# Four graph layers on one core: layer 3's q and k as seven block products, its attention one chunk further behind

## The chip, the core and the metric

The kernel runs on one core of a Trainium2 chip. The metric is the device time of one launch in microseconds, the median of several runs. In the profile the engines are PE (TensorE, matrix products; PEld is its loading of weights), DVE (VectorE), ACT (ScalarE), POOL (GpSimd) and SP (SyncE, which in this kernel only issues transfers). SBUF is the memory on the chip that all engines read and write, PSUM the eight banks into which TensorE writes its products, and DRAM the memory outside.

## What is computed

`x` is 128 batches x 64 tokens x 256 features, all float32. Four layers follow one another; each takes `h = max(layernorm(x), 0)` and adds its result to `x`. Layer 0 is a graph convolution with batch normalisation, layer 1 two graph convolutions and four small LSTMs. The change touches only layers 2 and 3:

```python
# layer 2: one head, causal, over the 64 tokens of a batch
q, k, v = split(h @ Wqkv)
scores = einsum('btd,bsd->bts', q, k) / sqrt(256) + adj_mask        # -1e30 above the diagonal
y = einsum('bts,bsd->btd', softmax(scores), v)
x = x + y @ Wo

# layer 3: four heads of 64, masked by the graph
q, k, v = (h @ W), cut into 3 parts and 4 heads
scores = einsum('bhid,bhjd->bhij', q, k) / sqrt(64) + mask          # mask: -inf where adj is 0
x = x + einsum('bhij,bhjd->bhid', softmax(scores), v)
```

## The kernel before

The 8192 tokens are 16 chunks of 512 (8 batches). Layers 0 and 1 end at 1545.8 us of the profiled execution; the rest is layers 2 and 3, chunk by chunk. They are made of small steps, Python functions in a table `steps`, each of which takes a chunk's number. The order of the work is written out by hand in strings: `FIRST` for chunks 0 to 2, `ROUND` for each of the chunks 3 to 12, `NORM` for 13 and 14, `LAST` for 15. `exp3-2` in a round for chunk c is the step exp3 of chunk c-2, `q2+0` the step q2 of chunk c. `run` (L1436) calls the steps in that order, and the schedule is manual: every engine, SP too, executes its instructions in the order of the string. An engine whose next instruction has to wait holds up all that stands behind it on that engine, while the others go on. Each kind of tile has a fixed number of buffers in a pool (two in pool `l2` where nothing else is said), and a step that takes the next buffer waits until the one before last has been read. All matrix products and transposes of layers 2 and 3 take their bank of PSUM from one ring of eight (`bank`), in the order of the calls.

Layer 2 of a chunk. Its two weights are folded ahead of time: `wqk_sb` is Wq times Wk transposed, so there is no k, and `wvo_sb` is Wv times Wo. The steps, with the engine and the name of their lines in the profile:

- load2: four transfers fetch the activations in channel layout (features on the partitions, tokens along).
- q2: four matmuls of 512 columns into two banks (L1108); ACT copies the first half of q to SBUF, DVE the second (copyq2).
- v2a, v2b: four matmuls of 256 columns each (L1101), an ACT copy each.
- score2: 16 small matmuls (L1191, tile 128x64); DVE scales, adds the mask, and takes the row maximum; POOL subtracts it (`shifted`, L1113). exp2 on ACT; divide2: sums, reciprocal and product on DVE.
- turn2: two transposes on TensorE (L1135) and an ACT copy. out2: 32 small matmuls (L1222, tile 64x32), and DVE adds the result to the residual `xs[c]`.
- keep: `put` sends `xs[c]` to DRAM; back reads it into another token order (four transfers), as layer 3's output will need it.

Layer 3 of a chunk:

- norm3: layer norm's statistics on DVE, then 1/sqrt on POOL. apply3: normalise and max on ACT. square3: DVE re-orders 32x32 squares, and a `put` and, in load3, four reads from DRAM complete the transposition into channel layout. chan3 does the same with eight TensorE transposes and two copies; it is used for chunks 0, 1 and 15, where no time lies between apply and use.
- q30, k30, q31, k31 (`qk3`, L1250): halves of q and k, two matmuls of 512 columns each into a bank of their own; ACT copies three of them to SBUF, DVE the fourth.
- v3a, v3b as in layer 2. score3: 32 matmuls of 64x64 into two banks (L1275); DVE masks them (L1281) and takes the maximum, POOL subtracts.
- exp3 on ACT, sum3 and divide3 on DVE, turn3: eight transposes and two ACT copies; out3: 32 matmuls of 64x64 into two banks (L1322). store: DVE adds the residual, and a transfer writes the chunk's result.

In `LAST` the last chunk's softmax and products go in two halves (names ending in a and b). A round of before is:

```python
ROUND = """exp3-2 q2+0 copyq2+0 sum3-2 load3-1 load2+1 v2a+0 divide3-2 score2+0 exp2+0 v2b+0 divide2+0
           turn3-2 q30-1 turn2+0 out3-2 out2+0 keep+0 norm3+0 k30-1 store-2 q31-1 back+0 apply3+0
           k31-1 v3a-1 square3+0 score3-1 v3b-1"""
```

so layer 3's projections and scores run one chunk behind layer 2, and its softmax and output two chunks behind. `NORM` is the same for chunks 13 and 14, whose followers come to layer 2 by norm2, apply2 and chan2 (on DVE, POOL, ACT and TensorE) in place of load2. `differences` (L671) belongs to the LSTMs: there a 2x2 block product is made of seven block matmuls, and POOL or DVE makes four differences of the operand's blocks for it. `put` (L231) uses a ring of four DRAM buffers for all of these trips.

## Time and profile before

| | us |
|---|---|
| median of 3 runs (lowest, highest) | 1932.98 (1932.7, 1933.74) |
| the profiled execution, whole | 1931.83 |
| its span, first to last instruction | 1929.9 |
| layers 0 and 1 | 0 to 1545.8 |
| layers 2 and 3 | 1545.8 to 1929.9, 384.1 |
| a steady round of them | 23.23 |
| LAST | 1879.92 to 1929.9, 49.98 |

How to read the lines that follow. The page's first part gives each engine's busy time, its share of the span and its number of instructions. `PEclk` shows the clock that TensorE was granted in 40 slices of the span, in tenths (9 is full or nearly so). A line of windows gives, for one stretch, its length, the busy time of each engine with the number of instructions, the granted clock, the share of the DMA engines' time and their GB/s. A line of the timeline gives the start, the duration, the engine, the line of the code, the operation with its tiles and shape, and the number of records taken together. Durations of neighbouring groups overlap a little, since matmuls are pipelined, so what a group costs is the step from its start to the next start.

### The profile page before, as it was taken

How to read it: one execution, taken by the hardware profiler on the slowest of the kernel's cores; microseconds unless marked ns; L12 is line 12 of the kernel's file. 1: busy time of each engine (PE TensorE's matmuls, PEld its weight loads, DVE VectorE, ACT ScalarE, POOL GpSimd, SP SyncE). 2: the span in 40 equal slices, each digit the busy share in tenths (PEclk: the TensorE clock that was granted, in tenths of full speed). 3: DMA queues.
4: the chain of work that ended last, by engine and by line, in shares of the span. 5: the costliest groups of instructions: out<-in, count | busy, mean ns of one | idle time of the engine just before them, and what ended most of it. 6: DMA issues, size and time to landing. Idle time of an engine off the chain costs nothing.

```text
span 1929.9 us, 37881 instructions
## 1 busy us (share of the span) xinstructions
PE 1911.8 (99%) x14827; PEld 1434.3 (74%) x14827; DVE 1140.6 (59%) x2985; ACT 950.3 (49%) x2120; POOL 371.8 (19%) x553
## 2 busy tenths in 40 slices
PE   9999999999999999999999999999999999999998
PEld 5444465897897898799689789878979966666666
DVE  6544354546557656655755755665555566666675
ACT  5654434445456455455545545545555544334443
POOL 3205210221211221121121121112112111111121
PEclk9999999999999999999999999999999999999999
DMA  4216712225424522531632452353134154444432
GB/s 137 63 35 223 282 44 68 81 83 170 148 83 157 182 84 70 188 106 70 213 115 83 165 174 83 132 178 112 58 131 147 51 153 122 136 138 136 143 114 81
DMA packets 109058, 238.23 MB, mean 123 GB/s; under 512 B 11216, under 2 KB 73168, under 8 KB 108880
## 3 DMA queue, kind: packets, MB, share of 16 engines
q1 hardware_dynamic: 108128, 234.47, 36.7%
q8 instruction: 117, 1.92, 0.4%
q0 software_dynamic: 320, 1.05, 0.2%
q14 instruction: 61, 0.50, 0.1%
q10 hardware_dynamic: 432, 0.30, 0.1%
HBM read 168.93 MB, written 66.85 MB: 122 GB/s over the span
## 4 chain that ended last, share of the span: by engine, by line
PE 96%; DVE 2%; ACT 1%; issue 0%; POOL 0%; DVEq 0%; POOLq 0%; ACTq 0%
PE x L829 22%; PE g L793 17%; PE z L829 11%; PE z L347 6%; PE v L1101 6%; PE y L829 6%; PE z L364 6%; PE p_q L1108 5%; PE p_k L1108 3%; PE u L574 3%; PE v L560 3%; PE agg_a L201 1%; PE agg_c L201 1%; PE s L1275 1%; PE o L1322 1%; PE tr L1135 1%
## 5 line engine op out<-in xcount | busy, mean ns | idle before, releaser
L838 DVE TENSOR_TENSOR gates<-gates,x 128x128 f32<-128x128 f32 (+2 forms) x384 | 119.6, 323 | 337.1 <-PE x L829 330.1
L829 PE MATMUL x<-xd,wset 128*128 128x128 f32 (+2 forms) x1280 | 285.2, 311 | 0.4 <-DVE gates L838 0.2
L829 PE MATMUL x<-hd,wset 128*128 128x128 f32 (+2 forms) x1152 | 246.8, 303 | 0.0
L829 PEld LDWEIGHTS x<-xd,wset 128*128 128x128 f32 x1280 | 202.1, 190 | 17.8 <-DVE gates L838 4.1
L721 ACT ACTIVATE gates<-gates,bias 128x256 f32<-128x256 f32 (+4 forms) x384 | 170.5, 491 | 67.1 <-DVE gates L838 64.2
L887 POOL TENSOR_TENSOR gates<-gates 128x512 f32<-128x512 f32 (+2 forms) x48 | 75.0, 1562 | 647.9 <-ACT gates L721 647.9
L829 PEld LDWEIGHTS x<-hd,wset 128*128 128x128 f32 x1152 | 185.1, 191 | 5.0
L772 ACT ACTIVATE gates<-g,bias 128x512 f32<-128x512 f32 (+2 forms) x240 | 138.1, 610 | 97.9 <-PE g L793 94.6
L793 PE MATMUL g<-hT,wset 128*128 128x256 f32 (+2 forms) x744 | 184.4, 405 | 1.1 <-DVE hT L732 1.1
L793 PEld LDWEIGHTS g<-hT,wset 128*128 128x128 f32 x744 | 140.5, 190 | 44.1 <-issue 8.8
L793 PE MATMUL g<-hT,wih 128*128 128x512 f32 x384 | 166.4, 592 | 0.0
L835 ACT COPY gates<-y 128x128 f32<-128x128 f32 (+2 forms) x192 | 54.2, 294 | 205.1 <-PE y L829 204.7
L829 PE MATMUL z<-hs,wset 128*128 128x128 f32 (+2 forms) x768 | 154.1, 303 | 0.0
L793 PEld LDWEIGHTS g<-hT,wih 128*128 128x128 f32 x384 | 72.3, 190 | 87.7 <-issue 83.2
L829 PEld LDWEIGHTS z<-hs,wset 128*128 128x128 f32 x768 | 119.8, 191 | 3.3
L347 PE MATMUL z<-agg,w_sb 128*128 128x512 f32 x256 | 114.1, 598 | 0.1
L364 PE MATMUL z<-h,w_sb 128*128 128x512 f32 x256 | 110.2, 592 | 0.0
L778 DVE TENSOR_TENSOR cell<-gates 128x512 f32<-128x512 f32 (+2 forms) x80 | 50.5, 648 | 101.0 <-ACT gates L772 100.9
L838 DVE TENSOR_TENSOR gates<-gates,z 128x128 f32<-128x128 f32 (+2 forms) x384 | 104.9, 317 | 0.1
L835 ACT COPY gates<-x 128x128 f32<-128x128 f32 (+2 forms) x192 | 56.6, 296 | 93.7 <-PE x L829 93.0
L721 ACT ACTIVATE gates<-x,bias 128x128 f32<-128x128 f32 (+2 forms) x192 | 74.8, 390 | 50.9 <-PE x L829 48.0
L829 PE MATMUL z<-hT,wset 128*128 128x128 f32 (+1 forms) x512 | 96.9, 301 | 0.0
(211 smaller groups left out, 3544.9 us busy)
## 6 DMA issues: line engine op xcount, KB each, us to landing
wset<-wfar SPq DMA_DIRECT2D x96, 960.0 KB, 6.4
hT<-far_h SPq DMA_DIRECT2D x116, 128.0 KB, 2.9
far_h<-hm SPq DMA_DIRECT2D x16, 512.0 KB, 3.4
far_n<-xs SPq DMA_DIRECT2D x16, 512.0 KB, 6.3
xs<-far_n SPq DMA_DIRECT2D x64, 128.0 KB, 3.6
far_x<-xs SPq DMA_DIRECT2D x16, 512.0 KB, 2.6
x<-far_x SPq DMA_DIRECT2D x64, 128.0 KB, 3.4
xt<-in_x_dram SPq DMA_DIRECT2D x15, 512.0 KB, 4.0
```

The source lines that it names most:

```text
L347: nc.tensor.matmul(ps, w1_sb[:, k, m * P : (m + 1) * P], agg[:, k, :], start=(k == 0), stop=(k == KD - 1))
L364: nc.tensor.matmul(banks[c, m], w2_sb[:, k, m * P : (m + 1) * P], h1[c][:, k, :], start=(k == 0), stop=(k == KH - 1))
L560: nc.tensor.matmul(banks[m], wg0_sb[:, k, m * P : (m + 1) * P], agg[:, k, :], start=(k == 0), stop=(k == KD - 1))
L721: nc.scalar.activation(gate(q, c, part), src, AF.Tanh if q == 2 else AF.Sigmoid, bias=bs[:, q * KD + c : q * KD + c + 1])
L772: nc.scalar.activation(columns_of(gate(q, c)), natural(banks[q, c][:, :n].rearrange("p (w b) -> p w b", b=nb)), AF.Tanh if q == 2 else AF. ...
L793: nc.tensor.matmul(banks[q, c][:, :n].rearrange("p (w b) -> p w b", b=nb)[:, w, :], block(q, c, k), hv[:, k, w.start * p : (w.stop - 1) * ...
L829: nc.tensor.matmul(folded(self.psum(kind)), wsets[p, self.q][:, BLOCKS[kind][i], :], (ox[self.s] if part == "x" else oh)[kind], start=firs ...
L835: nc.scalar.copy(gate(self.q, kind // 5, halves[kind // 5]), self.psum(kind))
L838: nc.vector.tensor_add(gate(self.q, *dst), gate(self.q, *a), self.psum(kind))
L887: nc.gpsimd.tensor_mul(gates[:, 0, :, :n], gates[:, 0, :, :n], gates[:, 2, :, :n])
L1101: nc.tensor.matmul(ps[:, i, :], hT[:, k, j, :], w[:, k, first : first + D], start=(k == 0), stop=(k == KD - 1))
L1108: nc.tensor.matmul(ps.rearrange("p (a n) -> p a n", n=P), w[:, k, m * P : (m + 1) * P], hT[:, k], start=(k == 0), stop=(k == KD - 1))
```

## The change

Three things change together.

1. Layer 3 runs one chunk further behind. In the round for chunk c, its softmax and output are those of chunk c-3, its q, k and v those of chunk c-2, and its scores those of c-2 at the round's end. The strings are re-written for that: FIRST ends earlier, `LAST` no longer contains layer 2 of chunk 15, and the steps stand in another order. In a round, layer 3's output products (out3) now stand directly ahead of its scores; norm3 is cut in two (norm3a, norm3b) with the statistics of two of the four tiles in each; back reads the chunk put two rounds before. chan3 remains for chunk 0 alone; chunks 1 and 15 go through DRAM (square3, load3) like the others. `put` has twelve DRAM buffers where it had four. The pool of layer 1's right side is closed after FIRST, and a pool `l3` with two buffers takes its place for layer 3's new tiles, its v among them.

2. q and k of chunks 1 to 14 are made by seven block products. The operand is cut into 2x2 blocks: two halves of the features by two halves of the tokens. POOL forms four differences of activation blocks per chunk (`sums_h`), and once four combinations of weight blocks (`ring_places`, after FIRST). Each product is two matmuls of 256 columns (one for q, one for k) that share an accumulating bank: products 1, 6, 7 and 4 go into a bank X one after the other, 5 and 3 into Y, 2 into Z. ACT copies X or Y to its place in `qk` after products 1, 5, 6 and 4, and DVE adds Z, Y and X to what stands there (c11, c12, qc). The order of the steps is

       qa   product 2 -> Z, product 1 -> X, ACT: copy X
       q5   product 5 -> Y, ACT: copy Y                       (after layer 2's transposes, turn2)
       c11  DVE: add Z
       qb   product 6 -> X, ACT: copy X, product 3 -> Y
       qc   product 7 -> X, DVE: add X
       c12  DVE: add Y
       qd   product 4 -> X, ACT: copy X

   Chunks 0 and 15 keep q30, k30, q31 and k31.

3. `LAST` holds what is left: attention of chunk 13, projections, scores and attention of chunks 14 and 15.

The diff, without unchanged context:

```diff
-    def put(mid, name, tag="far", bufs=4):
+    def put(mid, name, tag="far", bufs=12):
...
         for k in range(2):
             steps["qk"[k] + f"3{m}"] = lambda c, m=m, k=k: qk3(c, m, k)
+    l3 = []
+    def ring_places():
+        pool = l3[0]
+        l3.append(pool.tile([P, 2, 4, P], F32, tag="ws", name="ws3", bufs=1))
+        a = w3_sb[:, :, : 2 * D].rearrange("p k (i m f) -> p k m i f", i=2, m=KD)
+        d = l3[1].rearrange("p i s f -> p s i f")
+        for dst, x, y, op in ((0, a[:, 0, 1], a[:, 1, 1], OP.add), (1, d[:, 0], a[:, 0, 0], OP.subtract),
+                              (2, a[:, 0, 0], a[:, 0, 1], OP.subtract),
+                              (3, a[:, 1, 0], d[:, 1], OP.subtract)):
+            nc.gpsimd.tensor_tensor(d[:, dst], x, y, op)
+    @step
+    def sums_h(c):
+        hT = st[c, "hT3"]
+        t = l3[0].tile([P, 4, CH // 2], F32, tag="td", name=f"td_{c}", bufs=1)
+        t = [t[:, i, :].rearrange("p (a n) -> p a n", n=P) for i in range(4)]
+        b = {(k, j): hT[:, k, 2 * j : 2 * j + 2, :] for k in range(KD) for j in range(2)}
+        for f in differences(nc.gpsimd, t, b[0, 0], b[0, 1], b[1, 0], b[1, 1]):
+            f()
+        st[c, "o7"] = {1: b[0, 0], 2: b[1, 0], 3: b[1, 1], 4: t[3], 5: t[0], 6: t[1], 7: t[2]}
+    def seven(c, kind, tag):
+        first = (c, tag) not in st
+        if first:
+            st[c, tag] = bank(f"{tag}7_{c}")
+        for i in range(2):
+            m, k = {1: (0, 0), 2: (0, 1), 4: (1, 1)}.get(kind, (0, 0))
+            w = (w3_sb[:, k, i * D + m * P : i * D + (m + 1) * P] if kind in (1, 2, 4) else
+                 l3[1][:, i, {5: 0, 6: 1, 7: 2, 3: 3}[kind], :])
+            nc.tensor.matmul(
+                st[c, tag][:, i * CH // 2 : (i + 1) * CH // 2].rearrange("p (a n) -> p a n", n=P), w,
+                st[c, "o7"][kind], start=first and not i, stop=True, skip_group_check=True)
+    def part7(c, m, j):
+        return st[c, "qk"][:, :, m, j * CH // 2 : (j + 1) * CH // 2]
+    def bank7(c, tag):
+        return st[c, tag].rearrange("p (i n) -> p i n", i=2)
+    @step
+    def qa(c):
+        st[c, "qk"] = l3[0].tile([P, 2, KD, CH], F32, tag="qk", name=f"qk_{c}", bufs=1)
+        seven(c, 2, "Z")
+        seven(c, 1, "X")
+        nc.scalar.copy(part7(c, 0, 0), bank7(c, "X"))
+    @step
+    def q5(c):
+        seven(c, 5, "Y")
+        nc.scalar.copy(part7(c, 1, 1), bank7(c, "Y"))
+    @step
+    def c11(c):
+        nc.vector.tensor_add(part7(c, 0, 0), part7(c, 0, 0), bank7(c, "Z"))
+    @step
+    def qb(c):
+        seven(c, 6, "X")
+        nc.scalar.copy(part7(c, 0, 1), bank7(c, "X"))
+        seven(c, 3, "Y")
+    @step
+    def c12(c):
+        nc.vector.tensor_add(part7(c, 0, 1), part7(c, 0, 1), bank7(c, "Y"))
+    @step
+    def qc(c):
+        seven(c, 7, "X")
+        nc.vector.tensor_add(part7(c, 1, 1), part7(c, 1, 1), bank7(c, "X"))
+    @step
+    def qd(c):
+        seven(c, 4, "X")
+        nc.scalar.copy(part7(c, 1, 0), bank7(c, "X"))
+        st[c, "q3"], st[c, "k3"] = st[c, "qk"][:, 0], st[c, "qk"][:, 1]
+    @step
+    def norm3a(c):
+        t = [small.tile([P, NJ, i], F32, tag=f"ln_{i}_4", name=f"st{i}_n3_{c}") for i in (6, 2)]
+        st[c, "stats"] = t
+        stats_of(c, range(2))
+    def stats_of(c, tiles):
+        stats, mv = st[c, "stats"]
+        for j in tiles:
+            nc.vector.bn_stats(stats[:, j, :], xs[c][:, j, :])
+            nc.vector.bn_aggr(mv[:, j, :], stats[:, j, :])
+    @step
+    def norm3b(c):
+        stats_of(c, range(2, NJ))
+        mv = st.pop((c, "stats"))[1]
+        rstd = small.tile([P, NJ], F32, tag="ln_rstd4", name=f"rstd_n3_{c}")
+        rsqrt(rstd, mv[:, :, 1], EPS)
+        st[c, "n3"] = mv, rstd
     def scores(c):
         q, kk = st.pop((c, "q3")), st.pop((c, "k3"))
...
     def v3h(c, t):
         if not t:
-            st[c, "v3"] = l2.tile([P, NJ, D], F32, tag="v", name=f"v3_{c}")
+            pool = l3[0] if l3 else l2
+            st[c, "v3"] = pool.tile([P, NJ, D], F32, tag="v", name=f"v3_{c}")
         project_v(st[c, "v3"], st[c, "hT3"], w3_sb, 2 * D, f"3_{c}", [t])
     steps["v3a"] = lambda c: v3h(c, 0)
...
-    ROUND = """exp3-2 q2+0 copyq2+0 sum3-2 load3-1 load2+1 v2a+0 divide3-2 score2+0 exp2+0 v2b+0 divide2+0
-               turn3-2 q30-1 turn2+0 out3-2 out2+0 keep+0 norm3+0 k30-1 store-2 q31-1 back+0 apply3+0
-               k31-1 v3a-1 square3+0 score3-1 v3b-1"""
-    NORM = """exp3-2 q2+0 copyq2+0 sum3-2 load3-1 v2a+0 divide3-2 score2+0 exp2+0 v2b+0 divide2+0
-              turn3-2 norm2+1 q30-1 turn2+0 out3-2 out2+0 keep+0 apply2+1 norm3+0 k30-1 store-2 q31-1 back+0
-              apply3+0 k31-1 chan2+1 v3a-1 square3+0 score3-1 v3b-1"""
+    ROUND = """exp3-3 q2+0 copyq2+0 sum3-3 load3-1 sums_h-2 load2+1 v2a+0 divide3-3 score2+0 exp2+0 v2b+0
+               divide2+0 turn3-3 qa-2 turn2+0 q5-2 c11-2 out2+0 keep+0 norm3a+0 qb-2 back-2 qc-2 norm3b+0 c12-2
+               v3a-2 qd-2 apply3+0 out3-3 score3-2 store-3 square3+0 v3b-2"""
+    NORM = """exp3-3 q2+0 copyq2+0 sum3-3 load3-1 sums_h-2 v2a+0 divide3-3 score2+0 exp2+0 v2b+0 norm2+1
+              divide2+0 turn3-3 qa-2 turn2+0 q5-2 c11-2 out2+0 keep+0 norm3a+0 qb-2 apply2+1 back-2 qc-2
+              norm3b+0 c12-2 v3a-2 chan2+1 qd-2 apply3+0 out3-3 score3-2 store-3 square3+0 v3b-2"""
...
                exp2+0 q2+1 divide2+0 copyq2+1 load2+3 turn2+0 v2a+1 v2b+1 out2+0 keep+0 res1+14 res1+15
                score2+1 norm3+0 exp2+1 q2+2 divide2+1 copyq2+2 apply3+0 back+0 v2a+2 v2b+2 turn2+1
                score2+2 chan3+0 pair1+14 pair1+14 out2+1 keep+1 exp2+2 divide2+2 q30+0 k30+0 turn2+2
-               norm3+1 pair1+15 pair1+15 q31+0 k31+0 apply3+1 out2+2 keep+2 back+1 score3+0 v3a+0 v3b+0
-               chan3+1 exp3+0 sum3+0 divide3+0 norm3+2 q30+1 k30+1 q31+1 k31+1 turn3+0
-               apply3+2 score3+1 square3+2 out3+0 store+0 back+2 v3a+1 v3b+1"""
-    LAST = """q2+0 copyq2+0 load3-1 exp3-2 sum3-2 v2a+0 v2b+0 divide3-2 score2+0 exp2+0 v3a-2 v3b-2 divide2+0
-              turn3-2 turn2+0 q30-1 out2+0 keep+0 out3-2 norm3+0 store-2 k30-1 apply3+0 back+0 q31-1 k31-1
-              chan3+0 score3-1 q30+0 k30+0 exp3-1 sum3-1 q31+0 k31+0 divide3-1 score3h+0 v3a-1 v3b-1
-              exp3a+0 sum3a+0 turn3-1 exp3b+0 v3a+0 divide3a+0 out3-1 sum3b+0 divide3b+0 store-1 v3b+0
-              turn3a+0 turn3b+0 out3a+0 storea+0 out3b+0 storeb+0"""
+               norm3+1 pair1+15 pair1+15 q31+0 k31+0 apply3+1 out2+2 keep+2 square3+1 score3+0 norm3+2
+               v3a+0 load3+1 v3b+0 apply3+2 square3+2"""
+    LAST = """exp3-2 sum3-2 load3+0 divide3-2 qa-1 q5-1 c11-1 v3a-1 qb-1 c12-1 qc-1 turn3-2 out3-2 qd-1
+              q30+0 score3-1 store-2 back-1 k30+0 back+0 exp3-1 q31+0 k31+0 sum3-1 divide3-1 score3h+0
+              v3b-1 exp3a+0 sum3a+0 turn3-1 exp3b+0 v3a+0 divide3a+0 out3-1 sum3b+0 divide3b+0 store-1
+              v3b+0 turn3a+0 turn3b+0 out3a+0 storea+0 out3b+0 storeb+0"""
     assert (NCH, SUP) == (16, 2)
     def run(order, c):
...
                                      mybir.EngineType.Activation, mybir.EngineType.Pool,
                                      mybir.EngineType.SP}):
         run(FIRST, 0)
-        for c in range(3, NCH - SUP - 1):
+        close_l1r()
+        pool3, close_l3 = pool("l3", 2, "right")
+        l3.append(pool3)
+        ring_places()
+        run(ROUND.replace("exp3-3 q2+0 copyq2+0", "q2+0 copyq2+0 exp3-3"), SUP + 1)
+        for c in range(SUP + 2, NCH - SUP - 1):
             run(ROUND, c)
-        run(NORM, NCH - SUP - 1)
-        run(NORM.removesuffix("v3a-1 square3+0 score3-1 v3b-1") + "square3+0 score3-1", NCH - SUP)
+        for c in range(NCH - SUP - 1, NCH - 1):
+            run(NORM, c)
+        run(ROUND.replace("load2+1", "").replace("qd-2", "qd-2 sums_h-1"), NCH - 1)
         run(LAST, NCH - 1)
     close_l2()
     close_w2()
-    close_l1r()
+    close_l3()
     psum.pop()[2]()
```

## The prediction

> **What bounds the kernel now.** I read the page first, then busy time by windows over layers 2 and 3 (1545.8 us to the end), then TensorE's timeline of one round, then the groups of that round. From the page:

> ```profile
> span 1929.9 us, 37881 instructions
> PE 1911.8 (99%) x14827; PEld 1434.3 (74%) x14827; DVE 1140.6 (59%) x2985; ACT 950.3 (49%) x2120; POOL 371.8 (19%) x553
> PEclk9999999999999999999999999999999999999999
> ```

> TensorE is the bound and its clock is full. A busy share can hide waits, so the windows must say whether the rounds that change have any:

> ```profile
> core 0: us, PE busy (x) PEld busy (x) DVE busy (x) ACT busy (x) POOL busy (x), PEclk, DMA share, GB/s
> 1626.30:1649.53 23.23, 23.23 (x259) 15.10 (x259) 14.35 (x31) 9.15 (x17) 3.78 (x4) 1.00 0.45 137
> 1812.13:1835.36 23.23, 23.23 (x260) 15.10 (x259) 14.35 (x31) 9.15 (x17) 3.79 (x4) 1.00 0.49 142
> 1879.92:1925.40 45.48, 44.58 (x523) 29.77 (x522) 28.72 (x55) 17.84 (x33) 7.78 (x7) 1.00 0.25 83
> ```

> Every steady round is 23.23 us with TensorE busy for all of it; DVE has 9 us, ACT 14 and POOL 19 to spare. So TensorE work removed from a round shortens it. The last window, where rounds run out, already waits 0.9 us. One round on TensorE (start, us, instruction; the step from one start to the next is the price):

> ```profile
> 1635.22 1.88 PE L1108 MATMUL p_q<-hT,w_sb 128*128 128x512 f32 x4
> 1636.94 0.38 PE L1135 MATMUL tr<-ident,s 128*128 128x128 f32 x2
> 1637.25 1.16 PE L1322 MATMUL o<-v,att 64*64 64x64 f32 x64
> 1638.34 1.09 PE L1222 MATMUL o<-v,att 64*32 64x256 f32 x32
> 1639.37 1.98 PE L1108 MATMUL p_k<-hT,w_sb 128*128 128x512 f32 x4
> 1641.19 1.88 PE L1108 MATMUL p_q<-hT,w_sb 128*128 128x512 f32 x4
> 1642.90 1.88 PE L1108 MATMUL p_k<-hT,w_sb 128*128 128x512 f32 x4
> 1644.62 1.89 PE L1101 MATMUL v<-w_sb,hT 128*128 128x256 f32 x8
> 1646.44 1.16 PE L1275 MATMUL s<-k,q 64*64 64x64 f32 x64
> 1647.53 1.99 PE L1101 MATMUL v<-w_sb,hT 128*128 128x256 f32 x8
> ```

> Each f32 matmul leaves two records. Four records of 512 columns step 1.72 us (0.429 each). Behind or ahead of a group with small tiles (64*64, 64*32) about 0.1 is added: 1.82 where p_k follows them, 1.82 for eight v records before the scores.

> **The change, part by part** (minus is faster).

> 1. Block products. Before, q and k of a chunk are 8 matmuls of 512 columns: 16 records x 0.429 = 6.87 us. After, 14 of 256 columns: 28 records. The nearest row is v (256 columns, a weight load each): sixteen of them step 3.45 us at 1549.3 in the chain of waits, 0.2155 each, so 6.03 us. Gain 0.83 a chunk; 14 chunks (1 to 14; 0 and 15 keep the old way) give **-11.7**. Bounds: 0.2275 a record (eight in 1.82, with a switch inside) leaves 0.50 a chunk, -7.0; exactly half of 0.429 gives 0.86, -12.0. The sixteen-record row is nearest, as the new products stand among 128*128 work.

> 2. Transposes of layer 3's activations on TensorE for chunks 1 and 15 (chan3) go; a trip through DRAM takes their place (per chunk one put and four gets on SP, where the load of the next chunk waits behind them anyway). Their stretches were 1587.90 to 1589.29 (1.39, with a 0.35 wait) and 1902.16 to 1903.97 (1.81, two waits): **-3.2**.

> 3. Layer 3's output products now stand directly ahead of its scores, both 64*64. Five tile switches a round become four: 13 rounds x 0.1 = **-1.3**.

> 4. Filling the ring. The first block ends without chunk 1's q, k and scores, so TensorE comes early to chunk 3. From the old rows: v of chunk 0 ends at 1587.90; q2 3.44 and v2a 1.72 bring it to 1593.1, where score2 wants both halves of q. On the other side DVE's adds for chunk 2 end at 1584.70; then square3 of chunk 1 behind ACT's apply (1585.21) 1.42, masks 1.28, maximum 1.22, statistics 2.1: 1591.2. POOL's rstd 1.35, nmr 0.16, ACT's apply 2.08: 1594.8. Only then ACT's q copy (0.57), and on DVE square3 of chunk 2 (1.42) and copyq2 (0.69): 1597.0. TensorE waits about 3.9, in two pieces of some 2.4 and 1.5, as the copies are queued behind work of the next step. Overlap between neighbours takes some 0.2 off: **+3.7** (2.5 to 4.5).

> 5. Waits inside a steady round. The bank X takes products 1, 6, 7 and 4 in turn, each after the former was read. 7 behind 6: drain 0.17, ACT's copy 0.59, two hand-overs of 0.04, 0.84 in all; product 3 stands between, 4 records, 0.86: even. 4 behind DVE's add of 7: v3a between them is 1.72, DVE needs 0.9 and its queue (adds 1.28, half the statistics 1.07) is through by then. out2 behind att2's copy: ACT does X's copy first, ends 0.80 after product 1, then att2 0.38 with hand-over, 1.15; TensorE has transposes 0.22 and product 5 0.86: 0.07 short. 13 rounds: **+0.9** (0 to +4, if the even one falls the wrong way).

> 6. Added engine work beside this. ACT one copy a round more (0.59), DVE adds of 0.685 instead of one 0.69 copy (+1.4: 15.7 of 22.4 us), POOL four differences: rows of that shape are 725, 777, 922 and 780 ns, 3.2 us, so 7.0 of 22.4. They lie between POOL's shift for layer 3 and that for layer 2: score2's maximum comes some 9.3 us after the end of score3, the differences end near 7.7. Slack 1.6, cost 0. If that cover is gone, turn2 waits, and with it out2. SP gets no new transfers in a round; back no longer waits for the put just issued, and 12 buffers for puts remove a wait that the queue's rows don't show: 0. ring_places adds four POOL operations once (2.9), hidden under item 4's wait. First ring round (turn2 behind late exp2) and the two rounds with norm2: **+0.5** (0 to 1.5).

> 7. The drain. Call E the end of out2 of chunk 15. Adds 1.28, statistics 2.1, one add between them 0.69, rstd, nmr and apply 3.6: E+7.7. But DVE first does chunk 13's masks, maximum and store (3.8), which begin when score3 ends at E+7.3: E+11.1, transposes 12.5. The put takes 3.1 to 4.4 (SP rows: 1856.97 to 1860.05, 1810.37 to 1814.74), the four gets 1.3+2.8: chunk 15 is there at E+19.7 to 21. TensorE comes at E+19.3. Wait 0.8. Turn3 directly ahead of out3 in chunk 13, no cover for two copies of ACT: 0.6. Products 6 behind late copies 0.2; out3 of chunk 14 behind exp3a and two copies on ACT 1.3; score3h behind k's copy 0.3 more than the 0.25 it had. **+3.2** (+1.5 to +5).

> Sum: -11.7 -3.2 -1.3 +3.7 +0.9 +0.5 +3.2 = **-7.9 us**. The profiled execution took 1931.83 (span 1929.9, 1.9 around it), so 1923.9 in its terms; the median of the runs is 1.15 higher, so **1925.1**.

> [...] The longest idle stretch of TensorE in the old trace of these layers is 0.45 us, at a granted clock of 1.00 everywhere, even in the 4.4 us after the last product. [...] The row for POOL's 128x256 differences spans 451 to 1179 ns over shapes, 922 in the mean for the third. [...]

> **Rivals.**
> - *Slower: X's hand-overs bind.* One bank read by ACT, DVE and ACT again between four products. If item 5's even wait is late by the copy (0.84) and product 4 waits behind the statistics as well (0.9 more), the round loses 1.74 and the total is -7.9+13x1.74 = +14.7: 1947.7. It decides from 0.61 us a round (7.9/13). For it: no slack at product 7. Against: 1.72 us of v3a, and ACT idle 14 us of a round.
> - *No change or nearly: POOL.* If shift 2 is late, 0.5 a round, 6.5 in all: 1931.6. For it: the third difference's 922 ns; against: 1.6 of slack.
> - *Less: heavier ends.* Items 4, 6 and 7 at their upper ends (+4.5, +1.5, +5): -4.3, 1928.7; the same comes of a clock drop.
> - *More: the ends are covered.* Items 4 to 7 at their lower ends (2.5, 0, 0, 1.5): -12.2, 1920.8.
> - *The change doesn't do what it says:* excluded, the built kernel has 14 x 14 products at the new line and 16 of the 128 old ones.

> **How the numbers follow.** Forecast 0.60, heavier ends 0.15, more 0.12, POOL 0.07, X 0.06. 0.2% (3.9 us) is about what a measurement of this kernel can tell from no change: 1929.1 and 1936.8 are the bounds. Faster by over that: forecast, more and heavier ends, 0.87 less 0.02 at their edge, 0.85; same 0.09 (POOL and that edge), slower 0.06. Range 1920.8 to 1930.5: it leaves out X and most of POOL above, a little of "more" below.

> **What would show it.** Right: rounds near 22.4 us; block products at 215 ns a record; one wait of 2 to 4 us for score2 of chunk 3; two or three waits of about 1 in the last 40 us. Wrong: rounds over 22.9, idle TensorE ahead of product 7 or 4, out2 waiting for a late exp2, or PEclk below 9 after chunk 3.

## The result, and the profile after

The changed kernel takes **1926.99 us** (median of 4 runs, 1925.4 to 1927.46), the kernel before, in runs beside it, 1932.84: 5.9 us less, a ratio of 0.9971 with a 95% interval of 0.9956 to 0.9986. The forecast was 1925.1, in a range of 1920.8 to 1930.5. The middle of the interval is 0.3% faster and its upper end 0.14%, so the gain is real but its size is known only roughly. The time is 2 us behind the forecast; most of the experiments go after these 2 us.

The page after, engines and granted clock:

```profile
span 1924.8 us, 38314 instructions
PE 1901.9 (99%) x14979; PEld 1463.0 (76%) x14979; DVE 1158.4 (60%) x3019; ACT 958.4 (50%) x2132; POOL 413.0 (21%) x613
PEclk9999999999999999999999999999999999999999
```

The clock's row looks as before: a slice is 48 us long, and a digit of 9 hides a short fall. The profiled execution of after had one right at its start (3.4 us at half clock, at 13 us), so its layer 2 begins 0.93 us later, at 1546.60. The change has no part in that: of the 14 profiled executions of this document, five begin layer 2 at 1545.4 to 1545.7 us, three of them with the change, seven at 1546.4 to 1547.0, and two at 1547.5 and 1547.7. Stages are therefore compared from the start of layer 2, by the starts of layer 2's q on TensorE:

| stage | before | after | difference |
|---|---|---|---|
| first block, to q2 of chunk 3 | 57.14 | 42.22 | -14.92 |
| round of chunk 3 | 23.32 | 28.71 | +5.39 |
| rounds of chunks 4 to 12 (9) | 9 x 23.23 | 9 x 22.33 | -8.10 |
| rounds of chunks 13 and 14 | 44.65 | 46.92 | +2.27 |
| q2 of chunk 15 to the last output products | 44.35 | 53.70 | +9.35 |
| layers 2 and 3 | 378.53 | 372.52 | -6.01 |

First block, rounds 13 and 14 and the end must be read together, since the deeper ring moves work from the first to the last: -3.30. The steady rounds give -0.90 each. The round of chunk 3, which fills the ring, is 6.38 us longer than its neighbours.

Windows of after: the fill (three stretches), then a steady round; the column behind the engines is the granted clock:

```profile
1594.15:1597.57 3.42, 0.33 (x2) 0.19 (x2) 2.05 (x6) 3.42 (x7) 3.42 (x6) 0.91 0.00 0
1597.57:1599.48 1.91, 1.91 (x31) 1.79 (x31) 1.84 (x3) 0.30 (x1) 1.17 (x2) 0.50 0.72 283
1599.48:1603.05 3.57, 3.57 (x9) 2.75 (x9) 2.23 (x6) 0.42 (x1) 0.61 (x1) 0.50 0.43 141
1617.53:1639.86 22.33, 22.33 (x272) 17.10 (x271) 15.52 (x33) 9.84 (x18) 6.57 (x8) 1.00 0.49 143
```

TensorE waits for most of 3.4 us, and then runs at half clock. In the first stretch the mean of 0.91 means 0.6 us at half, so the clock fell at about 1596.95; it is back at about 1603.8, 6.8 us later. The same place in TensorE's timeline of after (idle time before a group in brackets, with what ended it), and behind the gap a steady round's block products:

```profile
1592.26 1.89 PE L1101 MATMUL v<-wvo_sb,hT 128*128 128x256 f32 x8
1596.50 0.33 PE L1191 MATMUL s<-hT,q 128*64 128x64 f32 x2 [2.35 <-ACT q L1169]
1597.57 1.97 PE L1191 MATMUL s<-hT,q 128*64 128x64 f32 x30 [0.74 <-DVE q L1174]
1599.48 3.78 PE L1101 MATMUL v<-wvo_sb,hT 128*128 128x256 f32 x8
1603.05 1.39 PE L1135 MATMUL tr<-ident,s 128*128 128x128 f32 x8
...
1626.61 1.03 PE L1297 MATMUL Z<-hT,w_sb 128*128 128x256 f32 x4
1627.48 1.03 PE L1297 MATMUL X<-hT,w_sb 128*128 128x256 f32 x4
1628.34 0.38 PE L1135 MATMUL tr<-ident,s 128*128 128x128 f32 x2
1628.56 1.03 PE L1297 MATMUL Y<-td,ws 128*128 128x256 f32 x4
1629.52 1.09 PE L1222 MATMUL o<-v,att 64*32 64x256 f32 x32
1630.54 1.13 PE L1297 MATMUL X<-td,ws 128*128 128x256 f32 x4
1631.51 1.03 PE L1297 MATMUL Y<-hT,ws 128*128 128x256 f32 x4
1632.37 1.11 PE L1297 MATMUL X<-td,ws 128*128 128x256 f32 x4
1633.32 1.89 PE L1101 MATMUL v<-w_sb,hT 128*128 128x256 f32 x8
```

The two waits are the forecast ones, 2.35 and 0.74. What was not in the sum is behind them: v2b steps 3.57 us where it stepped 1.83 in the next round, the scores 1.91 for 30 records, the transposes 1.23 against 0.87. In the steady round the products step 0.86 or 0.87 where a 128*128 group follows (0.216 a record), 0.96 where small tiles stand next to them, and product 7 (from 1632.37) steps 0.95, 0.08 more than its neighbours, at the place where X's copy was forecast to be just in time. The waits of TensorE in layers 2 and 3 of after, total, number and longest:

```profile
PE s L1191 <- ACT q L1169: 2.4, 1, 2.4
PE o L1424 <- ACT att L1139: 1.1, 2, 0.8
PE p_q L1108 <- DMA hT<-far_h: 0.8, 1, 0.8
PE s L1191 <- DVE q L1174: 0.7, 1, 0.7
PE o L1424 <- ACT att L1495: 0.3, 1, 0.3
```

The first and fourth are the fill; the others lie in the last 40 us.

### The profile page after: what moved, and what is told of

Read it like the earlier page. It is cut to its first block, busy times and chain, and to the rows that moved or that the text cites. A ratio compares the mean times of both kernels' runs of the same rounds, so it can differ in the third digit from the quotient of the medians.

```text
span 1924.8 us, 38314 instructions
## 1 busy us (share of the span) xinstructions
PE 1901.9 (99%) x14979; PEld 1463.0 (76%) x14979; DVE 1158.4 (60%) x3019; ACT 958.4 (50%) x2132; POOL 413.0 (21%) x613
## 3 DMA queue, kind: packets, MB, share of 16 engines
q8 instruction: 118, 1.93, 0.4%
## 4 chain that ended last, share of the span: by engine, by line
PE 94%; DVE 3%; ACT 1%; DMA 1%; issue 1%; POOL 0%; SPq 0%; DVEq 0%; ACTq 0%; POOLq 0%
PE x L829 22%; PE g L793 18%; PE z L829 11%; PE z L347 6%; PE y L829 6%; PE z L364 6%; PE v L1101 5%; PE p_q L1108 3%; PE u L574 3%; PE v L560 3%; PE X L1297 3%; PE Y L1297 1%; PE agg_a L201 1%; PE agg_c L201 1%; PE s L1191 1%; PE agg_b L201 1%
## 5 line engine op out<-in xcount | busy, mean ns | idle before, releaser
L829 PEld LDWEIGHTS x<-xd,wset 128*128 128x128 f32 x1280 | 202.1, 190 | 17.7 <-DVE gates L838 3.9
```

Source lines behind the costliest of these rows:

```text
L829: nc.tensor.matmul(folded(self.psum(kind)), wsets[p, self.q][:, BLOCKS[kind][i], :], (ox[self.s] if part == "x" else oh)[kind], start=firs ...
```

## The experiments

Each kernel is the changed one with the edit shown, except the one in the old ring, which starts from the kernel before, and those on LAST, which stand on the fill's new order. The kernel before ran beside each: 1932.1 to 1932.6 us.

### A filler ahead of the wait

```diff
     def score2(c):
+        if c == SUP + 1:
+            keep_busy(20, "d")
```

`keep_busy` issues transposes of the identity into a bank of their own.

> The changed kernel with 20 transposes of the identity on TensorE directly ahead of score2 of chunk 3, into a bank that nobody reads; 20 x 0.109 = 2.2 us, less than the 2.35 us that TensorE waits there. No wait is taken away: score2 can start no earlier. Theory (the wait costs the clock): the half-speed stretch of 6.8 us after the wait is gone; in it the scores took 1.91 us where 30 of them take 1.06 in the next round, the second half of v 3.57 against 1.82, the transposes 1.23 against 0.87, together 3.0 us, so 1927.0 becomes 1924.0 and the granted clock is 1.00 throughout layers 2 and 3. Rival (the transfers that start at 1597 us slow TensorE, whatever the clock's record says): the stretch stays slow and the time stays within 0.5 us of 1927.0.

Measured: 1925.42 us (1924.19 to 1926.61, 5 runs; ratio 0.9961, 0.9948 to 0.9975). TensorE's timeline of this kernel:

```profile
1594.91 2.35 PE L151 MATMUL idle_d<-ident 128*128 128x128 f32 x20
1597.43 0.33 PE L1193 MATMUL s<-hT,q 128*64 128x64 f32 x2 [0.17 <-ACT q L1169]
1598.51 1.15 PE L1193 MATMUL s<-hT,q 128*64 128x64 f32 x30 [0.74 <-DVE q L1174]
1599.59 2.00 PE L1101 MATMUL v<-wvo_sb,hT 128*128 128x256 f32 x8
```

The scores begin 7.68 us after their round's start (1589.75), exactly as in the changed kernel (1588.82 to 1596.50), and then everything runs at full speed. The round takes 26.22 instead of 28.71: the fall costs **2.5 us**, not 3.0, because the transposes behind it now wait 0.22 for the softmax, which the slow stretch had hidden. The rival, transfers that slow TensorE, falls: they are there as before (200 GB/s in the 5.5 us behind the second wait, 191 in the changed kernel). In whole times the gain is only 1.6 us and the ranges overlap; this profiled execution came later to layer 2 (at 1547.53 us, that of the changed kernel at 1546.60), so the 2.5 rests on the stage.

### Half the filler

The same with `keep_busy(10, "d")`.

> As the filler run, with 10 transposes instead of 20: 1.1 us of work, so 1.25 us of the first wait and the 0.74 of the second are left. What the first batch showed: stretches of 2.35 + 0.74 us, and of 1.83 + 0.75, less than half a microsecond apart, brought the half clock, and 1.38 and 0.75 that lie 2.8 us apart did not. Theory (what counts is the idle share of a stretch of some 3 us): 1.99 us idle in 2.4 lies between, and the clock may fall in a part of the executions; where it holds 1924.4, where it falls 1926 to 1927. Rival (a single stretch longer than some 1.5 us is what counts): it holds in all of them.

Measured: 1926.35 (1925.3 to 1927.31, 6 runs; ratio 0.9969, 0.9957 to 0.998). In the profiled execution TensorE waited 1.26 and 0.75 us, and the clock held, at 1.00 in each of the 18 us from 1590 on: that round took 26.19 us, as with the whole filler. Two other rounds of this execution were 0.9 and 1.15 longer than 22.33, with two stalls of TensorE among scores that the profile puts down to nothing ("issue", 1.4 in all), so the time says less than the profile. That 2.0 us idle out of 2.3 are too few is not shown by it. One execution in which the clock held settles neither theory nor rival. Length alone does not decide, though: of eleven waits of 1.91 us in the old-ring run below, six were followed by a fall.

### Removing the wait: another order for the fill

```diff
-               v3a+0 load3+1 v3b+0 apply3+2 square3+2"""
+               v3a+0 load3+1 v3b+0"""
...
-        run(ROUND.replace("exp3-3 q2+0 copyq2+0", "q2+0 copyq2+0 exp3-3"), SUP + 1)
+        run(ROUND.replace("exp3-3 q2+0 copyq2+0 sum3-3",
+                          "q2+0 copyq2+0 exp3-3 apply3-1 sum3-3 square3-1"), SUP + 1)
```

> The changed kernel with apply3 and square3 of chunk 2 moved out of the first block into the first round, apply3 behind exp3 of chunk 0 on ACT and square3 behind sum3 on DVE, so that the copies of q are no longer queued behind them. Theory (the queue makes the wait, the wait the clock): score2 of chunk 3 starts at once; what is late next is the attention's softmax, 0.7 us at the transposes of chunk 0 and about 1.2 at those of layer 2, instead of 3.1, so 1 us less waiting; no piece is near 2.3 us, the clock holds, 3.0 more: 1923.0. Rival (contention): 1 us less, 1926.

Measured: **1922.89** us (1921.74 to 1924.03, 5 runs; ratio 0.995, 0.9937 to 0.9962). Its timeline, with the waits as they now stand:

```profile
1595.14 1.20 PE L1191 MATMUL s<-hT,q 128*64 128x64 f32 x32
1596.27 1.99 PE L1101 MATMUL v<-wvo_sb,hT 128*128 128x256 f32 x8
1599.65 1.06 PE L1135 MATMUL tr<-ident,s 128*128 128x128 f32 x8 [1.38 <-DVE s L1126]
...
1603.19 0.41 PE L1135 MATMUL tr<-ident,s 128*128 128x128 f32 x2 [0.75 <-DVE s L1126]
```

3.09 us of waiting became 2.13, in pieces 2.8 us apart, and the clock stays: the round of chunk 3 takes 24.86, 3.85 less. The wait was one of queues (copies of q behind work of the next step), as the prediction's item 4 had it, and it could be moved.

### The deeper ring with the old products

Layer 3's q and k as q30, k30, q31, k31 in the new order, no differences and no weight sums:

```diff
-               divide2+0 turn3-3 qa-2 turn2+0 q5-2 c11-2 out2+0 keep+0 norm3a+0 qb-2 back-2 qc-2 norm3b+0 c12-2
-               v3a-2 qd-2 apply3+0 out3-3 score3-2 store-3 square3+0 v3b-2"""
+               divide2+0 turn3-3 q30-2 turn2+0 k30-2 out2+0 keep+0 norm3a+0 q31-2 back-2 norm3b+0
+               v3a-2 k31-2 apply3+0 out3-3 score3-2 store-3 square3+0 v3b-2"""
```

> The changed kernel with layer 3's q and k made the old way, eight products of 512 columns, and no differences on POOL; the deeper ring and the order of the edges stay. Theory (the gain is the block products', 0.84 a chunk, and the ring by itself gains only a tile switch and what chan3 cost): steady rounds of 22.33 + 0.84 = 23.2 us, the fill's waits and the clock's fall as in the changed kernel, 1927.0 + 14 x 0.84 = 1938.8, that is 6 us slower than the kernel before. Rival (the ring and the order do most of it): rounds of 22.7 or less, at most 1932.

Measured: 1935.71 us (1933.37 to 1938.04, 10 runs; ratio 1.0017, 1.0008 to 1.0026), slower than the kernel before. A steady round is 23.07 us, and TensorE's timeline shows what the block products replace:

```profile
1649.92 1.88 PE L1108 MATMUL p_q<-hT,w_sb 128*128 128x512 f32 x4
1651.64 0.38 PE L1135 MATMUL tr<-ident,s 128*128 128x128 f32 x2
1651.86 1.88 PE L1108 MATMUL p_k<-hT,w_sb 128*128 128x512 f32 x4
1653.67 1.09 PE L1222 MATMUL o<-v,att 64*32 64x256 f32 x32
```

So of the 0.90 a round, **0.74** is the products' (23.07 to 22.33) and **0.16** the order's (23.23 to 23.07). 14 chunks x 0.74 = 10.4 us, and 1927.0 + 10.4 = 1937.4, near the measured 1935.7. The two profiled executions differ by 10.7 us from layer 2's start to the last product (384.4 against 373.7). In the runs the difference is smaller: three of these ten have a mean granted clock of 0.999, which leaves no room for a fall of 6.8 us, and took 1933.4 to 1934.6. The deeper ring by itself, with its fill, costs more than its rounds gain.

### The block products in the old ring

The kernel before with the new steps in the place of its own, for chunks 2 to 13, in ROUND and NORM alike; `sums_h-1` stands behind load2 (in NORM behind load3), and the pool `l3` and the weight sums come behind FIRST as in the changed kernel:

```diff
-               turn3-2 q30-1 turn2+0 out3-2 out2+0 keep+0 norm3+0 k30-1 store-2 q31-1 back+0 apply3+0
-               k31-1 v3a-1 square3+0 score3-1 v3b-1"""
+               turn3-2 qa-1 turn2+0 q5-1 c11-1 out3-2 out2+0 keep+0 norm3+0 qb-1 store-2 qc-1 c12-1 back+0
+               apply3+0 v3a-1 qd-1 square3+0 score3-1 v3b-1"""
```

> The kernel before, its ring and order kept, with q and k of chunks 2 to 13 as seven block products (the new steps stand where q and k stood; the differences directly behind load2). Theory (the depth is needed): product 7 has only the third product ahead of it to cover X's copy, and ACT, DVE and POOL come late behind work of layer 2: two waits of 1 to 2.5 us a round, rounds of 25 to 26 us, 1933 + 11 x 2.5 = some 1960. Rival (the depth is not needed, block products alone do it): rounds of 22.4 us, 1933 - 12 x 0.84 = 1923, better than the changed kernel because it pays no longer fill and no DRAM trips at the ends.

Measured: 1983.86 us (1983.42 to 1988.86; ratio 1.0271, 1.0257 to 1.0285), slower still than expected: rounds of 24.7 to 29.3 us. The waits of TensorE in its layers 2 and 3:

```profile
PE s L1354 <- ACT qk L1339: 21.9, 12, 1.9
PE X L1295 <- DVE qk L1334: 9.7, 10, 1.0
PE tr L1135 <- DVE s L1126: 7.8, 7, 3.2
PE X L1295 <- ACT qk L1324: 4.3, 2, 2.2
```

The scores wait 1.9 us for ACT's last copy of q and k, product 4 (the second line) 1.0 for DVE's add, in twelve and in ten rounds; with these waits six stretches at half clock of 3.4 us each come in that execution. The same seven products that gain 0.74 a round in one order lose 4 in another. Other orders of the old ring were not tried, so it isn't shown that the depth is needed. What differs at the costliest wait is the order: in the changed kernel out3 (0.98 us) stands between product 4 and the scores, here nothing does.

### The fifth product ahead of layer 2's transposes

```diff
-    ... turn3-3 qa-2 turn2+0 q5-2 c11-2 out2+0 ...
+    ... turn3-3 qa-2 q5-2 c11-2 turn2+0 out2+0 ...
```

> The changed kernel with the fifth product, its copy and c11 ahead of layer 2's transposes instead of behind them, in all rounds. Theory (product 5 is the cover for ACT's copy of the transposes): behind the transposes TensorE goes directly to layer 2's output products, which need the copy: drain 0.17, copy 0.38, hand-overs, and product 5's copy of 0.59 is ahead of it on ACT, 0.9 to 1.1 us a round, 13 rounds: 1927.0 + 13 = 1940. Rival (ACT is idle 12 us of a round and the copy hides): 1927 within 2 us.

Measured: 1935.53 us (1933.64 to 1938.18, 10 runs; ratio 1.0017, 1.0008 to 1.0026); steady rounds 23.13. In its timeline:

```profile
1650.67 1.03 PE L1297 MATMUL Y<-td,ws 128*128 128x256 f32 x4
1651.54 0.38 PE L1135 MATMUL tr<-ident,s 128*128 128x128 f32 x2
1652.65 1.10 PE L1222 MATMUL o<-v,att 64*32 64x256 f32 x32 [0.73 <-ACT att L1139]
```

0.80 a round, where 0.9 to 1.1 was expected, for one step of 0.86 us on the wrong side of two transposes. Moving this one step back costs 8.5 us, more than the whole change gains.

### The differences made twice

```diff
-        for f in differences(nc.gpsimd, t, b[0, 0], b[0, 1], b[1, 0], b[1, 1]):
+        for f in 2 * differences(nc.gpsimd, t, b[0, 0], b[0, 1], b[1, 0], b[1, 1]):
```

> The changed kernel with POOL's four differences of every chunk made twice over, into the same places: 2.8 to 2.9 us more on POOL in each round. In the changed kernel POOL is idle for 2.19 us between the last difference and the shift of layer 2's scores, and the transposes of layer 2 come 0.77 us after the last product of its softmax. Theory (the slack is real, 3.0 in all): the shift is 0.7 late, that is taken up before the transposes: rounds of 22.3 to 22.5 us, 1927 to 1929. Rival (POOL is close to the bound, as the prediction's no-change case had it, or DVE and POOL hold each other up where both read SBUF): rounds of 23 us or more, 1936 or more.

Measured: 1938.95 us (1937.88 to 1939.66, 5 runs; ratio 1.0034, 1.0021 to 1.0046), rounds of 23.38: the rival's number. POOL's timeline in one round, and DVE's division (layer 3's softmax) of the same time:

```profile
1645.27 0.73 POOL L674 TENSOR_TENSOR td<-hT 128x256 f32<-128x256 f32 x1
1645.96 1.72 POOL L675 TENSOR_TENSOR td<-hT 128x256 f32<-128x256 f32 x1
1647.63 0.73 POOL L676 TENSOR_TENSOR td<-hT,td 128x256 f32<-128x256 f32 x1
```

```profile
1645.40 1.69 DVE L1126 TENSOR_TENSOR s<-s,rs 128x1024 f32<-128x1024 f32 x1
```

The slack was there, but the second half of the differences meets the division: the difference that overlaps it takes 1.72 instead of 0.73, the division 1.69 instead of 1.22. The shift is then 1.65 us late instead of 0.7, and layer 2's transposes wait 0.86. In the changed kernel the last difference ends at 1623.21 and the division begins at 1623.30: they miss each other by a tenth of a microsecond.

### The ends, and the buffers

Chunk 15's chan3 in place of the trip:

```diff
-    LAST = """exp3-2 sum3-2 load3+0 divide3-2 ...
-              q30+0 score3-1 store-2 ...
+    LAST = """exp3-2 sum3-2 divide3-2 ...
+              chan3+0 q30+0 score3-1 store-2 ...
...
-        run(ROUND.replace("load2+1", "").replace("qd-2", "qd-2 sums_h-1"), NCH - 1)
+        run(ROUND.replace("load2+1", "").replace("qd-2", "qd-2 sums_h-1").replace("square3+0 ", ""), NCH - 1)
```

> The changed kernel with chunk 15's activations turned on TensorE, eight transposes and two copies directly ahead of its q, in place of the trip through DRAM. Theory (the trip saves the transposes but is 0.75 late): the wait of 0.75 goes, the transposes cost 0.87 and the copy behind them 0.6 to 0.8 of waiting: 0.7 to 1.0 us more in the last stage, 1927.9. Rival (the trip is as dear as what it replaced): within 0.2 us in the last stage.

Measured: 1927.33 us (1926.48 to 1928.62, 8 runs; ratio 0.9973, 0.9963 to 0.9983). The last stage takes 54.19 us against 53.70: the trip gains 0.5, between theory and rival.

Four DRAM buffers (`bufs=4` in `put`):

> The changed kernel with four DRAM buffers for the trips in place of twelve. Theory (no transfer ever waited for a buffer): the rounds stay at 22.33 us and the time at 1927.0, within the 1.5 us that runs scatter. Rival (a put waits until the reads of four puts before have landed, and what is queued behind it on SP with it): chunk 15's trip or a load3 comes later and TensorE waits for it, over 1928.5.

Measured: 1926.69 us (1923.52 to 1927.63, 5 runs; ratio 0.9965, 0.9953 to 0.9977); rounds of 22.33, the last stage 53.73. The twelve buffers are worth nothing here.

### A new order for LAST

On top of the fill's order; the first edit below is its first half, the second its second half:

```diff
-    ... turn3-2 out3-2 qd-1 q30+0 score3-1 store-2 back-1 k30+0 ...
+    ... turn3-2 qd-1 out3-2 score3-1 store-2 q30+0 back-1 k30+0 ...
...
-    ... v3b-1 exp3a+0 sum3a+0 turn3-1 exp3b+0 v3a+0 ...
+    ... v3b-1 turn3-1 exp3a+0 sum3a+0 exp3b+0 v3a+0 ...
```

> The fill's order of the run before (1922.9 us) and a new order in LAST: product 4 of chunk 14 stands between chunk 13's transposes and its output products, the scores of chunk 14 directly behind these, then chunk 15's q; and the transposes of chunk 14 with their copies stand ahead of the first half of chunk 15's softmax. Theory (the waits at the end are queue waits, and moving covers them): of the 2.35 us that TensorE waits in the last 40 us of the changed kernel (0.24, 0.75, 0.25, 0.82 and 0.29) the 0.75 for chunk 15's trip, the 0.24 and part of the 0.82 go, and one tile switch of 0.1; a wait of up to 0.7 at product 4 comes, whose cover is now only the transposes: 1.0 to 1.5 us less, 1921.6. Rival (the end is bound by the chain of chunk 15 itself, trip, scores, softmax and output): the waits move behind one another and the time stays at 1922.9.

Measured, both halves: 1923.4 us (1922.7 to 1924.86, 5 runs; ratio 0.9955, 0.9941 to 0.9968), no better than the fill's order alone.

> The fill's order (1922.9 us) with the first half of the new LAST alone: product 4 of chunk 14 between chunk 13's transposes and output products, the scores of chunk 14 behind these, then chunk 15's q. Theory (each half gains by itself, and the 0.72 of the run with both was a stall of TensorE's queue that is not in the order): from the start of the transposes of chunk 13 to that of chunk 15's first k, 7.25 us in the changed kernel, 6.5 here, 0.7 less: 1922.2. Rival (the order makes the stall): 7.25 again, 1922.9 or more.

Measured, first half: **1922.02** us (1921.34 to 1922.97, 5 runs; ratio 0.9946, 0.9934 to 0.9959). Its timeline:

```profile
1892.73 1.10 PE L1297 MATMUL X<-td,w_sb 128*128 128x256 f32 x4 [0.34 <-DVE qk L1336]
...
1894.75 0.98 PE L1376 MATMUL s<-qk 64*64 64x64 f32 x52
1896.45 0.45 PE L1376 MATMUL s<-qk 64*64 64x64 f32 x12 [0.72 <-issue]
```

The waits for the trip and for the output's copy are gone, 0.34 comes at product 4, and a stall of 0.72 in the middle of the scores, which no event releases. It stood at the same record (52 of 64) in the run with both halves. From the transposes to chunk 15's first k it is 7.29 us, 7.25 in the changed kernel: the rival's number for the stage. The median lies 0.9 below the fill's order, but their ranges overlap; what the stage does not show is not claimed as a gain.

> The fill's order with the second half alone: the transposes of chunk 14 and their copies ahead of the first half of chunk 15's softmax. Theory (a wait is moved, not removed: the 0.82 at chunk 14's output goes, some 0.5 comes at chunk 15's): from the start of chunk 15's first k to the end of the last output product 18.04 us in the changed kernel, 17.74 in the run with both halves; 17.7 here, 1922.6. Rival (0.82 goes and nothing comes): 17.2.

Measured, second half: 1922.65 us (1921.33 to 1924.29, 5 runs; ratio 0.9948, 0.9935 to 0.9962); from chunk 15's first k to the end of its last product 17.85 us against 18.04, where 17.7 was expected. The wait of 0.82 at chunk 14's output is gone, 0.52 stands at chunk 15's second half.

All four kernels with the fill's order are faster than both the kernel before and the changed one, by 8.9 to 10.5 us and by 3.6 to 5.

## Why the prediction came out as it did

The direction and the mechanism were right, and the size was inside the range; the sum was -7.9 and the measured difference -5.9. Part of that nearness is luck: a clock drop of 2.5 us that stood in no term was partly paid for by terms that were too cautious (the order, the waits inside a round, the end).

- **Items 1, 3 and 5 (steady rounds)**: predicted -0.83 for the products, -0.10 for the tile switch, +0.07 for a wait: 22.37 us a round. Measured 22.33. That these agree is in part compensation. The products give 0.74, since three of the seven stand beside small tiles and step 0.96 or 0.97, not the 0.86 of the sixteen-record row, and product 7 comes 0.08 late; the order gives 0.16. The 0.07 was forecast ahead of out2, where no wait stands. The rival "X's hand-overs bind" is not there in this order. In the old ring it is, with 1.0 at product 4. The run with the fifth product moved shows item 5's other wait instead, out2 behind att2's copy.
- **Item 4 (the fill)**: waits of 2.4 and 1.5 predicted, 2.35 and 0.74 measured; with the filler, so at full clock, the round is 3.89 longer than its neighbours, against +3.7. Right in size, though the second wait was half of the forecast; the rest of the 3.89 is lost around the two gaps and in a wait of 0.22 at the transposes. **What failed is what came behind it**: a fall of the clock stood only in a rival ("the same comes of a clock drop"), and no row of the trace before shows such a fall or what it costs. It came, at 2.5 us. The row I trusted, a granted clock of 1.00 beside a longest idle stretch of 0.45 us, says nothing about 3.1 us of waiting in 3.4. When the clock fell, at about 1596.95, 2.35 + 0.12 us of that waiting had passed.
- **Item 6 (POOL)**: 3.2 us of differences and 1.6 of slack predicted; 2.9 and 2.19 measured, cost 0. In the changed kernel the differences and divide3 do not overlap, by 0.1 us. Where they meet, in the run with the differences made twice, both take longer (1.72 for 0.73 and 1.69 for 1.22).
- **Item 7 (the end)**: +3.2 predicted. Measured waits: 0.24 ahead of chunk 13's output (0.6 predicted), 0.75 for the trip (0.8), 0.82 at chunk 14's output (1.3), and at the last scores no more than the 0.25 of before (0.3 more). Too short for the list of waits, but in the steps, are 0.2 at product 6 (0.2; the v products ahead of it step 1.93 in place of 1.72) and 0.2 at the transposes of chunk 14 (not forecast; 2.05 in place of 1.83). 2.2 in all: oversized by 1.0.
- **Item 2 (chan3)**: -3.2 for two chunks. For chunk 15 the run with chan3 gives 0.5 net of the trip's 0.75 wait, 1.25 before it, where 1.81 was taken from the old trace: in the new order the transposes would cost less than they did. Chunk 1's share was not measured alone.
- **The sum again** with what was measured: products -0.74 x 14 = -10.4, order -0.16 x 13 = -2.1, item 2 about -2.6 (1.81 less 0.56 for chunk 15, chunk 1 as predicted), fill +3.9, clock +2.5, item 6's +0.5 (rounds 13 and 14 are 1.13 longer than a steady one, where that of before was 0.88 longer), end +2.2: -6.0, as by the stages. Chunk 1's share in it is the forecast one, so the agreement is a check, not a proof.

## What to carry to other kernels

When an engine at its bound gets a gap where it had none, price the gap and then the clock behind it: here 3.1 us of waiting cost 2.5 more, and twenty dummy transposes, or two steps moved in the queues of ACT and DVE, took that back. In a hand-ordered pipeline a new algorithm's gain is decided by what stands between a product and the copy of its bank: the same seven products were worth -0.74, -0.74 + 0.80 or some +4 us a round in three orders. And compare stages between marks in the trace, not whole times, where the effects are a few tenths.

## What the runs showed of the hardware

```profile
1707.69:1711.10 3.41, 1.50 (x66) 1.23 (x66) 1.42 (x4) 2.62 (x6) 0.00 (x0) 1.00 0.77 234
1711.10:1714.52 3.42, 3.42 (x9) 2.70 (x10) 2.51 (x3) 0.00 (x0) 0.79 (x1) 0.50 0.42 169
1680.39:1683.80 3.41, 1.61 (x36) 1.09 (x36) 1.76 (x6) 2.97 (x6) 0.00 (x0) 1.00 0.93 290
1683.80:1687.21 3.41, 3.31 (x42) 2.57 (x43) 2.58 (x4) 0.64 (x2) 0.00 (x0) 1.00 0.46 177
```

- The same code ran at different clocks in different executions. With four buffers, runs of a mean granted clock of 0.999 took 1923.5 and 1924.6 us, runs of 0.997 took 1926.7 to 1927.6; by estimate, one stretch of 6.8 us at half clock alone brings the mean to 0.998.
- In the run with the differences made twice, the POOL difference of 128x256 that overlaps layer 3's division on DVE took 1.72 us, where the others of the round took 0.72 or 0.73, and the division 1.69, where it takes 1.22 in the changed kernel.
- TensorE stalled for 0.72 us in the middle of a group of small matmuls (64*64, behind record 52 of 64) in the profiles of two kernels with the same order there, with nothing that the profile shows as its cause. What does it was not found.
